# Three cost estimates of a list scheduler: GpSimd's splits and ScalarE's second-norm scaling

## Chip, cores and metric

The kernel runs on one core of one Trainium2 chip. The metric is the device time of one execution in microseconds, as the median of several runs. PE is TensorE, DVE is VectorE, ACT is ScalarE, POOL is GpSimd, SP is SyncE, which here only issues DMAs.

## What is computed

The input is 16 sequences of 256 tokens with 128 features, fp32. Twelve layers of linear attention (no softmax) with 16 heads of 8 features run one after another, then a layer norm, one gated feed-forward with a hidden width of 384, and a second layer norm.

```python
for i in range(12):
    q, k, v = split(x @ Wqkv[i].T + bqkv[i], 3)           # 16 heads of 8
    att = einsum('bhqd,bhkd->bhqk', q, k) / sqrt(8)
    y = einsum('bhqk,bhkd->bhqd', att, v)
    x = y @ Wproj[i].T + bproj[i] + x
x = layernorm(x0 + x)
h = silu(x @ wg.T) * (x @ wu.T)                            # wg, wu, wd: int weights / 127
x = layernorm(x + h @ wd.T)
```

## The kernel before

The 16 sequences are handled as 8 pairs (512 tokens each, tiles of 128 partitions), in two halves of 4 pairs. Because there is no softmax, the attention of a layer is carried as a 128x128 matrix for each sequence (`tst`, with two more columns, so 2x130 = 260 columns for a pair). In each layer a pair goes through `products` (k, v and q by matmuls), `heads` (small 32x32 products for a whole half) and `projection`. fp32 operands are split for the matmuls into a rounded high part and a low remainder. In `projection` ACT writes the high part `hi` (L543), and POOL subtracts it to make the low part `lo` (L544); both go into `thl`. The next layer's matmuls L434 to L444 read both parts. The weights of each layer are split in the same way into `whl`, with the low part on POOL (L299).

After the layers, `ffn` runs for each pair. There is a first norm; the transposed tokens are split into `xh` and `xl`; `whole` (L694) adds them up again for the residual, on ACT or POOL. For each of three blocks of 128 hidden features, PE makes the gate and up products (L706, L707), ACT the SiLU (L709), and DVE the product with `up` (L710). The result is rounded into `hh` (L713, ACT or DVE), the remainder `hl` is taken (L714, POOL or DVE), and both go into the down product (L719, L720). Then DVE adds the residual (L732), PE transposes (L736), and the second norm follows: DVE statistics (L618, L621, L623), POOL's power -0.5 and one product (L634, L636), ACT's scaling, four chunks of 128 tokens for a pair (L650), and the store (L743). The last pair is cut in two: DVE scales its first two chunks (L648), ACT the other two.

No order is written out by hand. Every step is an `Op` with a cost in nanoseconds for each engine that may do it. `Plan.run` makes a list schedule when the kernel is built: it keeps a time at which each engine comes free, takes for every ready step the engine on which it would be finished first, and issues, among the steps that could start first, the one with the lowest priority number. A step's result counts as ready some time after its end (`AFTER`, `TO_PE`). In the feed-forward, DVE's finish is counted 500 ns later than it is (`SPARE`):

```python
rank = t + c + (SPARE if e == DVE and o.prio > L - 1.6 else 0)
```

The instructions go to each engine's queue in the order that this plan gives, and on the chip each engine works through its queue in that order. An estimate therefore does nothing on the chip by itself: it can only move a step to another engine or to another place in a queue. The costs that matter here:

```python
def dve(n, fast=False):
    return 69 + n / (1.92 if fast else 0.96)
def act(n, sbuf=False, pointers=0):
    return (94 if sbuf else 51) + 93 * pointers + n / 1.2
op({POOL: pool(N), DVE: dve(N)}, ... sub(e, t(hlo), t(sg), t(hh)) ...)      # L714, N = 512
op({ACT: act(N), POOL: pool(N)}, whole, ...)                                # L694
```

`pool(n)` is used by the split of the weights (n = 512, once 128), by `thl`'s low part (260, POOL only), by the mask product of `heads` (L511, 256, DVE or POOL), by `whole` and by `hl` (512).

Of the kernel before, what the change touches and what calls it, by code (L numbers as in the profile page):

```python
# [21 lines left out]
C = 128  # L22
# [13 lines left out]
K = N // 128  # L36
# [37 lines left out]
PE, ACT, DVE, POOL, SP = "pe", "act", "dve", "pool", "sp"  # L74
# [100 lines left out]
# [6 lines that stand above are left out]


def pool(n):
    return 147 + 2.1 * n


def flat(t):
# [4 lines left out]
def linear_attention_ffn_kernel(ctx: ExitStack, tc: tile.TileContext, x, xt, wall, wq0, bias, wg, wu, wd, out):  # L192
# [86 lines left out]
    def prep_weights(l):  # L279
# [17 lines left out]

        after = [vlo[G - 1]] if l > 1 else []
        plan.op({POOL: pool(n)}, lambda e: sub(e, whl[hl.slot][:, 1, a:], wraw[raw.slot][:, a:], whl[hl.slot][:, 0, a:].bitcast(F32)), [raw, *after], [hl], prio)  # L299

        def turn(e):
# [176 lines left out]
    def heads(l, o, prio, riders):  # L478
# [26 lines left out]
        for lo, oo, _, pc, _ in more:  # L505
# [3 lines left out]
        plan.op({DVE: dve(OB * 32)}, lambda e: nc.vector.tensor_tensor(  # L509
            gm, bank(pm)[:, : OB * 32].rearrange("p (b j) -> p b j", j=32), kvo[:, o * OB : (o + 1) * OB], ALU.add), [pm, vkvo[o]], [vgm[o]], prio)  # L510
        plan.op({DVE: dve(OB * 32), POOL: pool(OB * 32)}, lambda e: mul(e, gm, gm, mask32.unsqueeze(1).to_broadcast([128, OB, 32])), [], [vgm[o]], prio)  # L511

        def mm_y(e):
# [7 lines left out]
    def projection(l, p, py, prio):  # L521

        _, whv, turned = wts[l]
        bs, r = slice(p * PB, (p + 1) * PB), p % G
        wp = lambda i: wpt[turned.slot][:, i, r - 1, :] if r else whl[whv.slot][:, i, 3 * C :]
        hi, lo, ts = thl[p][:, 0], thl[p][:, 1], flat(tst[:, bs, :])
        yh, yl = yhl[p][:, 0], yhl[p][:, 1]
        pw = Val("bank")
        plan.op({ACT: act(PB * W), DVE: dve(PB * W)}, lambda e: copy(e, yh, bank(py)[:, : PB * W]), [py], [vyh[p]], prio)
        plan.op({DVE: dve(PB * W)}, lambda e: nc.vector.tensor_tensor(yl, bank(py)[:, : PB * W], yh.bitcast(F32), ALU.subtract), [py, vyh[p]], [vyl[p]], prio)  # L530

        def mm_w(e):
            o = bank(pw)[:, : PB * W]
            nc.tensor.matmul(o, wp(1), yh, start=True, stop=False)  # L534
            nc.tensor.matmul(o, wp(0), yh, start=False, stop=False)  # L535
            nc.tensor.matmul(o, wp(0), yl, start=False, stop=(l < L - 1))  # L536
            if l == L - 1:
                nc.tensor.matmul(o, centerr, flat(hi), start=False, stop=False)
                nc.tensor.matmul(o, centerr, flat(lo), start=False, stop=True)
        plan.op({PE: (3 if l < L - 1 else 5) * mmr(PB * W)}, mm_w, [vyh[p], vyl[p], vhi[p], vlo[p], whv, turned], [pw, vw[p]], prio)  # L540
        plan.op({DVE: dve(PB * W)}, lambda e: nc.vector.tensor_tensor(ts, bank(pw)[:, : PB * W], ts, ALU.add), [pw], [vt[p], vc[p]], prio)  # L541
        if l < L - 1:
            plan.op({ACT: act(PB * W, True)}, lambda e: copy(e, flat(hi), ts), [vt[p], vc[p]], [vhi[p]], prio)  # L543
            plan.op({POOL: pool(PB * W)}, lambda e: sub(e, flat(lo), ts, flat(hi).bitcast(F32)), [vt[p], vc[p], vhi[p]], [vlo[p]], prio)  # L544
# [50 lines left out]
    def ffn(p, prio):  # L595
# [5 lines left out]
        v = {n: Val() for n in ("tt", "st", "rs", "x1", "xh", "xl", "sg0", "sg1", "hh0", "hh1", "hl0", "hl1")}  # L601

        def op(costs, emit, reads, writes):
            plan.op(costs, emit, reads, writes, prio)

        def norm(src, centred, other=None):


            xs, rows = t("x1"), lambda: bank(src)
            cut = lambda a, k: a[:, k * C : (k + 1) * C]  # L610
            row = lambda k: cut(bank(other if other and k >= K // 2 else src), k)

            def stats(e, ks=range(0, K, 2)):

                for k in ks:
                    b = bank(other if other and k else src)
                    both = b[:, k * C : (k + 2) * C].rearrange("p (k c) -> p c k", c=C)
                    nc.vector.bn_stats(t("st")[:, k : k + 2, :].rearrange("p k s -> p (k s)"), both)  # L618

            def var(e):  # L620
                nc.vector.tensor_scalar(t("ve"), t("st")[:, :, 2], 1.0 / C, EPS, ALU.mult, ALU.add)  # L621
                if not centred:
                    nc.vector.tensor_scalar(t("nm"), t("st")[:, :, 1], -1.0, None, ALU.mult)  # L623
            some, tiny = dve(2 * C) + 40, 75 * (2 - centred)
            if other:
                parts = [Val(), Val()]
                for k, b in ((0, src), (2, other)):
                    op({DVE: some}, lambda e, k=k: stats(e, [k]), [b], [parts[k // 2]])
                op({DVE: tiny}, var, parts, [v["st"]])
            else:  # L630
                op({DVE: K // 2 * some + tiny}, lambda e: (stats(e), var(e)), [src], [v["st"]])

            def rstd(e):
                nc.gpsimd.tensor_tensor(t("rs"), t("ve"), mhalf, ALU.pow)  # L634
                if not centred:
                    nc.gpsimd.tensor_tensor(t("nb"), t("nm"), t("rs"), ALU.mult)  # L636
            op({POOL: 1060 + 220 * (not centred)}, rstd, [v["st"]], [v["rs"]])

            def scale(e, ks=range(K)):
                if centred and e == DVE:  # L640
                    nc.vector.tensor_tensor(chunks(xs), chunks(rows()), t("rs").unsqueeze(2).to_broadcast([128, K, C]), ALU.mult)
                    return
                for k in ks:
                    d, r, rs = cut(xs, k), row(k), t("rs")[:, k : k + 1]
                    if centred:
                        nc.scalar.activation(d, r, AF.Copy, scale=rs)
                    elif e == DVE:
                        nc.vector.tensor_scalar(d, r, t("st")[:, k, 1:2], rs, ALU.subtract, ALU.mult)  # L648
                    else:
                        nc.scalar.activation(d, r, AF.Identity, bias=t("nb")[:, k : k + 1], scale=rs)  # L650
            if centred:
                costs = {DVE: dve(N), ACT: K * act(C, False, 1)}
            else:
                costs = {ACT: K * act(C, False, 2)}
            if not other:
                op(costs, scale, [src, v["rs"], v["st"]], [v["x1"]])
                return [v["x1"]]

            ends = [Val(), Val()]
            op({DVE: 2 * 319}, lambda e: scale(e, range(2)), [src, v["rs"], v["st"], v["x1"]], [ends[0]])  # L660
            op({ACT: 2 * act(C, False, 2)}, lambda e: scale(e, range(2, K)), [other, v["rs"], v["st"], v["x1"]], [ends[1]])
            return ends


# [7 lines left out]
        def mm_r(e):  # L672
            rows = cqs[p // G].unsqueeze(1).to_broadcast([128, 2, C])
            for b in range(PB):
                nc.tensor.matmul(bank(pr)[:, 2 * b * C : 2 * (b + 1) * C], pick[:, p % G * PB + b, :], rows, start=True, stop=False)
                for k in (2 * b, 2 * b + 1):
                    nc.tensor.matmul(bank(pr)[:, k * C : (k + 1) * C], x[:, k * 128 : (k + 1) * 128], t("tt")[:, b * C : (b + 1) * C], start=False, stop=(k % 2 == 1))
        op({PE: K * mm32() + PB * mmr(2 * C)}, mm_r, [vx[p], v["tt"], vcq[p // G], vpick], [pr])
        norm(pr, True)

        def tr_x(e):
# [48 lines left out]
        for (d, cols), o, r in zip(downs, outs, sums):  # L730
# [6 lines left out]
            op({PE: m // 128 * 109}, tr_o, [r], [o])  # L737
        po, po2 = outs if len(outs) == 2 else (*outs, None)
        ends = norm(po, False, po2)
        m = N // len(ends)  # L740
        for i, end in enumerate(ends):
# [59 lines left out]
```

## Time and profile before

| what | value |
|---|---|
| median of 3 runs | 305.5 us (305.44 to 306.06) |
| the profiled execution's own time | 305.16 us |
| its span, first to last instruction | 303.2 us |
| mean granted TensorE clock | 0.998 |
| busy in the span: PE | 294.3 us (97%) |
| DVE | 226.1 us (75%) |
| ACT | 217.7 us (72%) |
| POOL | 137.8 us (45%) |
| chain of work that ended last | PE 87%, DVE 10%, ACT 1%, issue 1% |

The span is what the instructions of one profiled execution cover; the execution's own time is 1.96 us longer than the span. The busy shares are means over stages with different limits: start (about 0 to 30 us), layers (to about 240 us), feed-forward (to about 298 us) and a last stretch without matmuls.

### The profile page before, as it was taken

How to read it: one execution, taken by the hardware profiler on the slowest of the kernel's cores; microseconds unless marked ns; L12 is line 12 of the kernel's file. 1: busy time of each engine (PE TensorE's matmuls, PEld its weight loads, DVE VectorE, ACT ScalarE, POOL GpSimd, SP SyncE). 2: the span in 40 equal slices, each digit the busy share in tenths (PEclk: the TensorE clock that was granted, in tenths of full speed). 3: DMA queues.
4: the chain of work that ended last, by engine and by line, in shares of the span. 5: the costliest groups of instructions: out<-in, count | busy, mean ns of one | idle time of the engine just before them, and what ended most of it. 6: DMA issues, size and time to landing. Idle time of an engine off the chain costs nothing.

```text
span 303.2 us, 12834 instructions
## 1 busy us (share of the span) xinstructions
PE 294.3 (97%) x5376; PEld 269.8 (89%) x5376; DVE 226.1 (75%) x683; ACT 217.7 (72%) x559; POOL 137.8 (45%) x208
## 2 busy tenths in 40 slices
PE   8999999999999999999999999999999999999981
PEld 8989999999999999999999999989999998878760
DVE  4796887777677676876767777786644789999993
ACT  3556877867777768777686666777887558788875
POOL 8256452334531445225432354224431167777883
PEclk9999999999999999999999999999999999999999
DMA  7624213112031120311302102120000000000225
GB/s 214 163 91 131 67 39 89 38 46 82 3 89 37 39 89 4 88 40 28 98 2 56 37 17 50 49 68 17 2 2 4 3 1 2 0 0 8 63 70 138
DMA packets 22489, 15.65 MB, mean 52 GB/s; under 512 B 1952, under 2 KB 19872, under 8 KB 22432
## 3 DMA queue, kind: packets, MB, share of 16 engines
q1 hardware_dynamic: 21872, 14.62, 17.3%
q8 instruction: 42, 0.69, 0.9%
q10 hardware_dynamic: 560, 0.22, 0.3%
q14 instruction: 15, 0.12, 0.1%
HBM read 8.02 MB, written 2.10 MB: 33 GB/s over the span
## 4 chain that ended last, share of the span: by engine, by line
PE 87%; DVE 10%; issue 1%; ACT 1%; POOLq 0%; POOL 0%; DVEq 0%
PE bank L455 14%; PE bank L434 8%; PE bank L517 8%; PE bank L436 7%; PE bank L435 7%; PE bank L442 5%; PE bank L499 5%; PE bank L536 4%; PE bank L534 4%; PE bank L535 4%; PE bank L443 3%; PE bank L444 3%; PE bank L336 3%; DVE st L618 2%; PE bank L706 2%; PE bank L707 2%
## 5 line engine op out<-in xcount | busy, mean ns | idle before, releaser
L210 POOL TENSOR_TENSOR thl<-tst,thl 128x260 fp32r<-128x260 f32 x88 | 64.8, 768 | 123.1 <-ACT thl L205 123.1
L205 ACT COPY qgv<-bank 128x256 f32<-128x256 f32 x169 | 59.8, 378 | 19.2 <-PE bank L444 12.9
L205 ACT COPY kv<-bank 128x512 f32<-128x512 f32 (+1 forms) x93 | 53.4, 575 | 19.5 <-PE bank L436 14.2
L434 PE MATMUL bank<-whl,thl 128*128 128x256 f32 x176 | 51.9, 295 | 0.0
L436 PE MATMUL bank<-whl,thl 128*128 128x256 f32 x176 | 49.7, 282 | 0.0
L435 PE MATMUL bank<-whl,thl 128*128 128x256 f32 x176 | 49.4, 281 | 0.0
L455 PE MATMUL bank<-kv,g 128*128 128x128 f32 x352 | 46.1, 275 | 0.0
L541 DVE TENSOR_TENSOR tst<-bank,tst 128x260 f32<-128x260 f32 x96 | 36.9, 425 | 9.4 <-PE bank L536 9.0
L205 ACT CAST thl<-tst 128x260 fp32r<-128x260 f32 x88 | 33.0, 408 | 14.6 <-DVE tst L541 14.5
L455 PEld LDWEIGHTS bank<-kv,g 128*128 128x128 f32 x352 | 42.7, 191 | 0.4 <-issue 0.4
L448 DVE TENSOR_SCALAR qgv<-bank,bcol 128x2 f32<-128x2 f32 x88 | 19.2, 221 | 28.3 <-ACT qgv L205 22.9
L434 PEld LDWEIGHTS bank<-whl,thl 128*128 128x128 f32 x176 | 33.1, 188 | 4.0 <-issue 3.8
L530 DVE TENSOR_TENSOR yhl<-bank,yhl 128x260 fp32r<-128x260 f32 x96 | 34.4, 420 | 2.2 <-ACT yhl L205 2.1
L436 PEld LDWEIGHTS bank<-whl,thl 128*128 128x128 f32 x176 | 33.1, 188 | 0.3 <-POOL thl L210 0.2
L435 PEld LDWEIGHTS bank<-whl,thl 128*128 128x128 f32 x176 | 33.2, 189 | 0.0
L442 PE MATMUL bank<-thl,whl 128*128 128x260 f32 x88 | 28.8, 327 | 0.0
L205 ACT CAST yhl<-bank 128x260 fp32r<-128x260 f32 (+1 forms) x61 | 21.8, 408 | 8.3 <-PE bank L517 7.7
L207 DVE CAST yhl<-bank 128x260 fp32r<-128x260 f32 (+1 forms) x43 | 16.7, 430 | 12.7 <-PE bank L517 12.7
L517 PE MATMUL bank<-qgv,gm 32*32 32x130 f32 x1536 | 25.8, 280 | 0.2 <-DVE gm L213 0.2
L443 PE MATMUL bank<-thl,whl 128*128 128x260 f32 x88 | 24.8, 282 | 0.0
L444 PE MATMUL bank<-thl,whl 128*128 128x260 f32 x88 | 24.7, 281 | 0.0
L517 PEld LDWEIGHTS bank<-qgv,gm 32*32 32x32 f32 x1536 | 17.2, 103 | 5.5 <-ACT kv L205 0.3
(157 smaller groups left out, 694.7 us busy)
## 6 DMA issues: line engine op xcount, KB each, us to landing
wraw<-wall SPq DMA_DIRECT2D x12, 256.0 KB, 3.0
wpt<-whl SPq DMA_DIRECT2D x24, 96.0 KB, 2.2
qgv<-x SPq DMA_DIRECT2D x8, 256.0 KB, 5.0
xt<-xt SPq DMA_DIRECT2D x8, 256.0 KB, 3.1
out<-kv SPq DMA_DIRECT2D x7, 256.0 KB, 2.3
wpt<-whl SPq DMA_DIRECT2D x24, 64.0 KB, 2.7
wpt<-whl SPq DMA_DIRECT2D x24, 32.0 KB, 1.9
wraw<-wg SPq DMA_DIRECT2D x1, 192.0 KB, 3.2
```

The costliest lines, as they stand in the source:

```text
L205: nc.scalar.copy(dst, src)
L210: (nc.vector if e == DVE else nc.gpsimd).tensor_tensor(dst, a, b, ALU.subtract)
L434: nc.tensor.matmul(o, hi[:, b, 0:C], hl(0, 1, 2), start=True, stop=False)
L435: nc.tensor.matmul(o, hi[:, b, 0:C], hl(1, 1, 2), start=False, stop=False)
L436: nc.tensor.matmul(o, lo[:, b, 0:C], hl(0, 1, 2), start=False, stop=True)
L442: nc.tensor.matmul(o, hl(0, 0), flat(hi), start=True, stop=False)
L443: nc.tensor.matmul(o, hl(0, 0), flat(lo), start=False, stop=False)
L444: nc.tensor.matmul(o, hl(1, 0), flat(hi), start=False, stop=True)
L455: nc.tensor.matmul(bank(pgv)[:, b * C : (b + 1) * C], g0[p][:, b, :], tv(b), start=True, stop=True)
L517: nc.tensor.matmul(bank(pys[r])[group(g + r), b * W : (b + 1) * W], gm[group(g), r * PB + b, :], qss[p][group(g), b, :], start=True, stop= ...
L530: plan.op({DVE: dve(PB * W)}, lambda e: nc.vector.tensor_tensor(yl, bank(py)[:, : PB * W], yh.bitcast(F32), ALU.subtract), [py, vyh[p]], [ ...
L541: plan.op({DVE: dve(PB * W)}, lambda e: nc.vector.tensor_tensor(ts, bank(pw)[:, : PB * W], ts, ALU.add), [pw], [vt[p], vc[p]], prio)
```

## The change

It replaces the straight line that stands for POOL's two-input splits by another one, and the estimate of ACT's scaling in the second norm, `act(128, False, 2)` = 343.7 ns a chunk, by 375 ns, and by 400 ns for the two chunks of the last pair. No step is added, removed or rewritten.

```diff
 def pool(n):
-    return 147 + 2.1 * n
+    return 135 + 2.4 * n
...
             else:
-                costs = {ACT: K * act(C, False, 2)}
+                costs = {ACT: K * 375}
...
             op({DVE: 2 * 319}, lambda e: scale(e, range(2)), [src, v["rs"], v["st"], v["x1"]], [ends[0]])
-            op({ACT: 2 * act(C, False, 2)}, lambda e: scale(e, range(2, K)), [other, v["rs"], v["st"], v["x1"]], [ends[1]])
+            op({ACT: 2 * 400}, lambda e: scale(e, range(2, K)), [other, v["rs"], v["st"], v["x1"]], [ends[1]])
```

## The prediction, made before the changed kernel was run

> **What bounds the kernel now.** I read the page's busy slices first, then the busy time by stage, then the chain that ended last over the final 17 us, then GpSimd's own order there.
>
> The busy slices, 7.6 us each, in tenths:
>
> ```profile
> PE   8999999999999999999999999999999999999981
> DVE  4796887777677676876767777786644789999993
> POOL 8256452334531445225432354224431167777883
> ```
>
> PE is full from the second slice on. DVE joins it only in the last eight slices, and there POOL is no longer half idle. The same by stage (the stretch, then PE, PE's weight loads, DVE, ACT and POOL):
>
> ```profile
> 30.00:240.00 210.00, 209.84 (x4542) 196.61 (x4541) 150.04 (x465) 154.45 (x407) 78.75 (x109) 1.00 0.16 43
> 240.00:286.50 46.50, 46.11 (x281) 39.24 (x280) 44.22 (x97) 35.90 (x86) 32.00 (x32) 1.00 0.03 8
> 286.50:298.00 11.50, 9.60 (x53) 7.09 (x51) 11.10 (x32) 9.61 (x24) 9.61 (x13) 1.00 0.32 88
> 298.00:303.20 5.20, 0.00 (x0) 0.00 (x0) 0.74 (x3) 1.67 (x5) 1.21 (x2) 0.87 0.55 151
> ```
>
> In the layers PE is idle 0.16 us of 210 at a full clock. No new order can gain there, and one that keeps PE fed loses nothing. From 240 to 286.5 us PE is idle 0.39 us. After that the binding engine changes: DVE is busy 11.10 of 11.50 us, PE only 9.60. The chain says so in words (start, duration, what):
>
> ```profile
> 286.63 1.28 DVE xt L710 x2
> 287.91 0.60 DVE xt L732
> 288.51 0.68 DVE st L618 x2
> ...
> 289.62 0.52 DVE hl L210
> 290.14 0.68 DVE qgv L710
> 290.82 0.60 DVE hl L210
> 291.42 0.60 DVE xt L732
> ```
>
> One DVE instruction follows the other; a 128x512 one advances the chain by 0.60 us. Two of these links are `hl` remainders that could as well have been POOL's. So the end is paid in DVE instructions: one more of 128x512 in this stretch costs 0.60 us, one less gains as much until PE or ACT is late. ACT's last run of scaling there is 12 chunks in 4.58 us from 294.29, ends at 298.87, and ACT then waits 0.47 us for POOL: it is the next one late, by half a microsecond.
>
> **What the estimates say, and what the chip does.** The groups of the split and of the scaling (min/median/max in ns for the tile queries of `hl` and of the scaling):
>
> ```profile
> L210 POOL TENSOR_TENSOR hl<-xt,hh x8: 1288/1300/1732, 255.2 to 287.0; 128x512 fp32r<-128x512 f32 x8
> L210 POOL TENSOR_TENSOR hl<-qgv,hh x7: 1279/1304/1684, 259.5 to 291.5; 128x512 fp32r<-128x512 f32 x7
> L210 DVE TENSOR_TENSOR hl<-xt,hh x7: 676/681/1801, 260.8 to 290.7; 128x512 fp32r<-128x512 f32 x7
> ```
>
> At 512 elements POOL takes 1300 ns. The old estimate, 147 + 2.1*512 = 1222, is 78 short; the new one, 135 + 2.4*512 = 1364, is 64 too long. At 260 elements the old one gives 693 and the new one 759; four of these splits in a row take 3.03 us in the layers (127.02 to 130.05), 757 each. So the new line follows the trace in the layers, where nothing depends on it, and in the feed-forward it only trades one error for an equal one of the other sign.
>
> **The change, part by part.** It adds and removes no instruction. Its cost on the chip is what the list does with it.
>
> *thl's low parts, 88 on POOL alone, 66 ns dearer each.* Four in a row are counted 264 ns later. In a steady layer the fourth ends at 130.05 and the first k, v product of the next layer starts at 130.68, 0.63 us after it; 264 fits into that, so PE's order there should stay. What covers it is the other half's q products (128.13 to 130.2); if that cover were gone, the price would be 0.26 us a half. Only at the first layer, where four splits take 3.32 us from 22.31 and PE works right behind them (9.78 of 10 us busy between 20 and 30), can the order change: between -0.22 (that idle time filled) and +0.26 (264 ns waited once). I take nothing.
>
> *The weights' low parts (142 dearer, POOL alone) and the mask product (685 to 749, DVE at 336 or POOL).* The weights are split a layer ahead, with POOL idle 5 us and more around them (5.61 us before 127.02): nothing. The mask product's 4 that are on POOL could go to DVE, 435 ns each at 75% load: nothing.
>
> *ACT's second-norm scaling: 4*343.7 = 1375 becomes 1500, and 687 becomes 800.* The trace has 1.50 us for four and 4.58 for twelve, 0.81 for the last two: the new estimates are right. No other engine may do this step, so only what stands behind it in ACT's list moves: 125 ns later a pair. ACT is busy 9.61 of 11.5 us at the end and waits for POOL there. Between -0.1 and +0.1 by order; I take nothing.
>
> *hl's remainders and `whole`, 142 dearer each.* This is the part that can move work. DVE's due is 69 + 512/0.96 = 602, plus the handicap of 500: with both engines free, POOL at 1222 loses to 1102, and wins where DVE is taken for some time. I carried the list's rule through with the old costs: POOL's lead over DVE in its 15 remainders is 204 ns at least. So 142 alone moves none. Where two stand back to back, the second is charged 284. That is so at one place, as GpSimd's order in time shows:
>
> ```profile
> 286.83 0.20 POOL L636 TENSOR_TENSOR nb<-nm,rs 128x4 f32<-128x4 f32 x1
> 286.98 1.29 POOL L210 TENSOR_TENSOR hl<-xt,hh 128x512 fp32r<-128x512 f32 x1
> 288.22 1.30 POOL L210 TENSOR_TENSOR hl<-qgv,hh 128x512 fp32r<-128x512 f32 x1
> ```
>
> There the list's lead for the second was 205 ns, less than 284: it goes to DVE. 288 us lies inside the DVE-bound end, so it adds a link to the chain: +0.60 us. It can cost more. A DVE remainder has two inputs in SBUF, and one of them met POOL:
>
> ```profile
> 260.80 1.80 DVE L210 TENSOR_TENSOR hl<-xt,hh 128x512 fp32r<-128x512 f32 x1
> 260.77 1.28 POOL L693 TENSOR_TENSOR kv<-yhl,thl 128x512 f32<-128x512 f32 x1
> ```
>
> It took 1.80 us for 0.68, and the next DVE instruction started 1.72 us after it instead of 0.60. So a moved remainder costs 0.60 at least and 1.72 if POOL happens to start just before it; I take 0.60, since 7 of the 8 on DVE ran at 676 to 693.
>
> The Trainium skill, "SBUF — State Buffer", section "Who interferes with whom", states this as a rule: a DVE instruction with two SBUF inputs contends with a GpSimd one that reads SBUF, and the later one blocks fully. It speaks against the change: at a busy POOL it would price the moved remainder at the 1.72 of the pair above, and the sum would be +1.7.
>
> *Sum.* The profiled execution took 305.16 us (span 303.2 and 1.96 around it); with +0.60 it would take 305.76. The median of the runs is 0.34 above the profiled execution, so I forecast 306.1.
>
> **The rivals.**
>
> *Given back (not slower).* With the remainder of 288.22 gone, POOL is free 1.3 us earlier, and the next remainder, which DVE does at 290.74, may come back to POOL: in the list DVE had it by only 115 ns, while DVE itself is now 602 later. Then DVE has as many links as before: 305.5, between 305.2 and 305.9. For it: the small lead. Against it: that one belongs to the last pair, 1.30 us on POOL where DVE needs 0.68, and POOL's idle time before 291.55 is short. It decides if the list's ready time of that remainder lies within about 0.6 us of POOL's.
>
> *Faster.* `whole` at 260.77 was POOL's by 305 ns in the list, directly behind a remainder: it is now charged 284, so 21 ns more of any delay send it to ACT, which stands idle 1.59 us until 266. Then the 1.80 us of DVE become 0.68: -1.12 on DVE. Of that PE can use only its 0.39 idle us before 286.5; the rest counts if DVE keeps the lead to the end. Time: 305.5 less 0.4 to 1.1, 304.4 to 305.1.
>
> *Two links or a blocked one.* Besides the one above, `hh` casts (ACT or DVE, 0.43 on DVE) lean to DVE as ACT is counted dearer; two remainders give +1.2, one with a blocked one 0.60 + 1.72 = 2.3: 306.7 to 307.8.
>
> *PE starved.* A later due of `hl` lets PE take other products first, and they hold the eight PSUM banks; the down product then comes late. PE has no spare time before 286.5, so each wait counts in full; beyond 307.8.
>
> **How the numbers follow.** A measurement of this kernel can tell about 0.2% (0.6 us) from no change, so the border lies at 306.1. One link on DVE: 0.28, of which 0.18 over the border and 0.10 under it. Two or a blocked one: 0.17. Starved PE: 0.07. Given back: 0.24. Faster: 0.24. That gives slower 0.18 + 0.17 + 0.07 = 0.42, same 0.10 + 0.24 = 0.34, faster 0.24. The range from 304.4 to 307.8 takes in all but the starved case and what the faster case holds below its price. The likeliest case's own range is 305.9 to 306.5.
>
> **What would show it.** Right: the layers take the same time (PE idle under 0.3 us between 30 and 240); 14 `hl` remainders on POOL and 9 on DVE, the new one near 288 us; DVE over 11 us busy of the last 11.5 before its final statistics, which come 0.6 us later. Wrong: 15 and 8 as before (given back); `whole` once instead of twice on POOL and no DVE remainder above 1 us (faster); PE idle by more than 0.5 us between 240 and 286 us, or a layer that lost its cadence of about 9.7 us a half, which would refute the reasoning on the layers.

## The result, and the profile after

The changed kernel takes 306.76 us (median, 305.8 to 307.66) against 305.51 us for the kernel before, measured in turns: a ratio of 1.004 with a 95% interval from 1.0027 to 1.0053. It is slower by 1.25 us. The forecast was 306.1 us with a range from 304.4 to 307.8.

The busy slices of the profile after (the span is 304.9 us):

```profile
PE   8999999999999999999999999999999999999971
DVE  4796777777777676776767777786544789999993
POOL 8255353334541345314442254323431176767783
```

The picture is the same as before. By stage (the stretch, then PE, PE's weight loads, DVE, ACT and POOL; the third stretch starts 0.3 us later, as the end does, and stops where POOL's last power starts, 298.02 before and 299.71 now):

```profile
30.00:240.00 210.00, 209.66 (x4537) 196.23 (x4535) 150.68 (x464) 153.62 (x404) 78.92 (x109) 1.00 0.16 43
240.00:286.80 46.80, 46.41 (x294) 39.44 (x282) 44.16 (x97) 36.24 (x86) 32.28 (x33) 1.00 0.03 8
286.80:299.70 12.90, 10.01 (x53) 7.09 (x51) 12.49 (x32) 9.77 (x25) 9.65 (x13) 1.00 0.28 79
299.70:304.90 5.20, 0.00 (x0) 0.00 (x0) 0.73 (x3) 1.58 (x5) 1.21 (x2) 0.70 0.55 151
```

PE is idle 0.34 us of 210 in the layers (0.16 before) and 0.39 us from 240 on, as before. From the last power on, the same 5.2 us follow. The third stretch, 11.50 us before, is 12.90 now. DVE is busy in it for 12.49 us, with the same 32 rows as before. So the time is in the DVE-bound end, and it isn't in more instructions. The `hl` remainders:

```profile
L210 POOL TENSOR_TENSOR hl<-xt,hh x8: 1281/1302/1748, 255.5 to 290.0; 128x512 fp32r<-128x512 f32 x8
L210 POOL TENSOR_TENSOR hl<-qgv,hh x7: 1283/1303/1687, 259.8 to 293.2; 128x512 fp32r<-128x512 f32 x7
L210 DVE TENSOR_TENSOR hl<-xt,hh x7: 674/684/1800, 261.1 to 292.5; 128x512 fp32r<-128x512 f32 x7
L210 DVE TENSOR_TENSOR hl<-qgv,hh x1: 691/691/691, 273.3 to 273.3; 128x512 fp32r<-128x512 f32 x1
```

15 on POOL and 8 on DVE, as before. But they are not the same ones. In the chain that ended last (start, duration, what) stands, 17 us before the end, a remainder that was not on DVE before:

```profile
287.57 1.59 DVE hl L210
289.16 0.60 DVE xt L710
289.76 0.60 DVE xt L732
290.36 0.68 DVE st L618 x2
...
292.57 0.61 DVE hl L210
...
293.26 0.60 ACT xt L709
293.86 1.41 ACT kv L650 x4
...
295.30 0.64 PE bank L736 x4
```

The other 128x512 links on DVE still advance it by 0.60. This one took 1.59. The timeline after, DVE and POOL (start, duration, engine, line, what; in brackets idle time and what ended it):

```profile
287.32 1.29 POOL L210 TENSOR_TENSOR hl<-qgv,hh 128x512 fp32r<-128x512 f32 x1
287.57 1.59 DVE L210 TENSOR_TENSOR hl<-xt,hh 128x512 fp32r<-128x512 f32 x1
...
289.99 1.30 POOL L210 TENSOR_TENSOR hl<-xt,hh 128x512 fp32r<-128x512 f32 x1 [1.38 <-ACT hh L205]
...
293.19 1.28 POOL L210 TENSOR_TENSOR hl<-qgv,hh 128x512 fp32r<-128x512 f32 x1
293.88 0.62 DVE L621 TENSOR_SCALAR ve<-st 128x4 f32<-128x4 f32 x1
```

Each of the two long DVE instructions begins inside a split of POOL's and ends 0.03 to 0.55 us after it: 0.91 us over the usual 0.68, and 0.45 over the variance's usual 0.17. Before, POOL's two splits of 286.98 to 289.52 (shown in the prediction) stood over these:

```profile
286.63 1.28 DVE L710 SCALAR_TENSOR_TENSOR xt<-bank,xt 128x512 f32<-128x512 f32 x2
287.83 0.68 DVE L732 SCALAR_TENSOR_TENSOR xt<-bank,kv 128x512 f32<-128x512 f32 x1
288.43 0.75 DVE L618 BATCH_NORM_STATS2 st<-bank 128x6 f32<-128x256 f32 x2
289.21 0.34 DVE L621 TENSOR_SCALAR ve<-st 128x4 f32<-128x4 f32 x1
...
289.54 0.68 DVE L210 TENSOR_TENSOR hl<-xt,hh 128x512 fp32r<-128x512 f32 x1
```

Those that read a PSUM bank kept their time; the variance, which reads SBUF alone, took 0.34 for 0.17; the remainder came just behind the splits. The Trainium skill, "SBUF — State Buffer", section "Who interferes with whom", says which is which: a DVE instruction with two SBUF inputs contends with a GpSimd one that reads SBUF, `tensor_scalar` can too in its two-port mode, and one with at most one SBUF input outside these modes does not. The rows agree: L210 at 0.68 or 1.59, L621 at 0.17 or 0.62 (in which mode it ran no row tells), the whole profile before has no 128x512 instruction of L710 or L732 above 0.693, and none of L618 above 0.433.

**Why the remainders changed places.** `Plan.run` can be followed without the chip. The pairs are counted from 0, so pair 7 is the last. With the old estimates, ACT's cast of pair 5's last block ends at 287.623 us in the list's time, and its remainder could start 0.160 later, at 287.783, before POOL comes free at 287.887. Both it and pair 6's remainder could then start there, and pair 5, being earlier, went first. With scaling at 1500 ahead of it, and all else as it was, the cast ends 125 ns later, and its remainder is ready at 287.908: 21 ns too late (with the new line for POOL too, both times are 66 ns later and the 21 ns the same). POOL takes pair 6's. Pair 5's goes to DVE, and later another one of pair 6's goes from DVE to POOL: an exchange. In the list with the new scaling estimates alone, these two are the only ones of 1906 steps that change engine. On the chip there is no such 21 ns: in the profile after, pair 5's cast ended at 287.18, before POOL came free at 287.37.

**A measure for the runs.** The profiles' starts differ (an unchanged layer program reaches the feed-forward between 244.8 and 246.7 us), so profiles are compared from the first variance instruction (L621) to the end of the span; and POOL's last six powers (L634) mark the DVE-bound part, without the last scalings and stores: from the first to the last of them 12.35 us before (285.67 to 298.02) and 13.70 after (286.01 to 299.71). The difference, 1.35, is 0.91 + 0.45 - 0.09 (an earlier variance took 0.25 for 0.34) + some 0.1 in the last transposes.

### The profile page after: what moved, and what is told of

It reads as the page before. It is cut to its first block, busy times and chain, and to the rows that moved or that the text cites. A ratio compares the mean times of both kernels' runs of the same rounds, so it can differ in the third digit from the quotient of the medians.

```text
span 304.9 us, 12847 instructions
## 1 busy us (share of the span) xinstructions
PE 294.8 (97%) x5376; PEld 269.9 (89%) x5376; DVE 228.6 (75%) x684; ACT 217.5 (71%) x557; POOL 138.2 (45%) x209
## 4 chain that ended last, share of the span: by engine, by line
PE 79%; DVE 15%; ACT 2%; issue 2%; POOLq 0%; DVEq 0%; POOL 0%; ACTq 0%
PE bank L455 14%; PE bank L517 8%; PE bank L434 8%; PE bank L435 7%; PE bank L436 7%; PE bank L442 5%; PE bank L499 5%; PE bank L536 4%; PE bank L534 4%; PE bank L535 4%; PE bank L443 3%; PE bank L444 3%; DVE xt L710 3%; PE bank L336 3%; DVE st L618 2%; DVE hl L210 2%
## 5 line engine op out<-in xcount | busy, mean ns | idle before, releaser
L210 POOL TENSOR_TENSOR thl<-tst,thl 128x260 fp32r<-128x260 f32 x88 | 64.6, 766 | 123.7 <-ACT thl L205 123.7
```

The lines of the kernel that those rows point to most:

```text
L210: (nc.vector if e == DVE else nc.gpsimd).tensor_tensor(dst, a, b, ALU.subtract)
```

## The experiments

Medians in us, beside those of the kernel before in the same series. The last two columns are the two measures just given.

| run | median | before | ratio (95%) | first variance to end | first to last power |
|---|---|---|---|---|---|
| before | | | | 58.4 | 12.35 |
| after | 306.76 | 305.51 | 1.004 (1.0027 to 1.0053) | 59.8 | 13.70 |
| e1 splits' line alone | 305.78 | 305.88 | 0.9991 (0.9977 to 1.0005) | 58.4 | 12.37 |
| e2 scaling alone | 307.14 | 305.88 | 1.004 (1.0025 to 1.0055) | 59.8 | 13.71 |
| e10 the same, another series | 307.1 | 305.71 | 1.0049 (1.003 to 1.0067) | 59.7 | 13.71 |
| e6 375 alone | 306.87 | 305.56 | 1.0044 (1.0028 to 1.006) | 59.8 | 12.27 |
| e7 400 alone | 305.51 | 305.56 | 1.0 (0.9982 to 1.0017) | 57.7 | 12.37 |
| e12 exchange alone | 307.64 | 305.76 | 1.0059 (1.0038 to 1.008) | 60.3 | 14.00 |
| e11 exchange undone | 306.65 | 305.76 | 1.0033 (1.0016 to 1.005) | 59.3 | 13.21 |
| e3 remainder later | 307.49 | 305.88 | 1.0048 (1.003 to 1.0065) | 59.8 | 13.72 |
| e5 later still | 306.75 | 305.56 | 1.005 (1.0031 to 1.0069) | 59.3 | 13.27 |
| e9 no wait left | 306.48 | 305.71 | 1.0025 (1.001 to 1.004) | 59.2 | 12.27 |
| e4 sum on ACT | 305.49 | 305.88 | 0.9987 (0.9969 to 1.0005) | 58.3 | 12.36 |
| e8 `nm` on POOL, sum on ACT | 305.23 | 305.56 | 0.9987 (0.9973 to 1.0001) | 58.0 | 12.09 |

The fifth column, less before's 58.4, follows the medians' differences within 0.4 us in all but e7, whose one profile is 0.7 us shorter than before's where its median shows no gain.

### Which estimate: e1, e2, e10

```diff
 def pool(n):
-    return 147 + 2.1 * n
+    return 135 + 2.4 * n      # e1: this alone
...
-                costs = {ACT: K * act(C, False, 2)}
+                costs = {ACT: K * 375}      # e2, e10: these two alone
-            op({ACT: 2 * act(C, False, 2)}, ...
+            op({ACT: 2 * 400}, ...
```

> Only GpSimd's estimate is new (135+2.4n); ScalarE's scaling keeps 343.7 ns a chunk. The list then gives the layers in the order of the changed kernel and the last 20 us in the order of the kernel before. My theory now: the loss lies in the last 20 us and comes from ScalarE's estimate, so this run is within 0.4 us of before (the changed trace was 0.09 us late after 70 us and 0.34 us late at 245 us): 305.3 to 305.9. The prediction's own step, that GpSimd's dearer splits move a remainder at the end, would make it 0.6 us or more slower.

> Only ScalarE's scaling estimate is new (375 and 400); GpSimd keeps 147+2.1n. The layers are those of before, instruction by instruction; at the end a remainder of pair 5 goes from GpSimd to VectorE and one of pair 6 from VectorE to GpSimd, as in the changed kernel. My theory: all of the loss, +1.0 to +1.4 us (306.5 to 306.9), final statistics about 1.3 us later, pair 5's remainder on VectorE near 287 us taking about 1.6 us. Rival (the layers' new order or GpSimd's estimate costs it): within 0.3 us of before.

The splits' line alone is no change that can be told; the scaling alone costs as much as the whole change. In e2 the long remainder (1.58 us) and the long variance (0.62) are there as in the profile after. e10 repeats it in another series:

> The kernel with ScalarE's estimate alone once more, for a comparison on the same chip in the same call: 306.6 to 307.2, ratio 1.003 to 1.005 by every theory.

### Which of the two scalings: e6, e7

e6 keeps the 375 alone, e7 the 400 alone.

> Only the estimate of 375 ns is new, the last pair's chunks keep 343.7. By its instruction order this kernel has the same exchange near 288 us (pair 5's remainder on VectorE, pair 6's on GpSimd) and a slightly different order before it. Theory of the exchange: slower by 1.0 to 1.4 us, 306.7 to 307.4. Rival (any new order at the end costs about the same, or the 400 is what costs): unlike that.

> Only the estimate of 400 ns for the last pair's two chunks is new. The order changes at 263 to 280 us, but the exchange near 288 us is not there: pair 5's remainder stays on GpSimd, pair 6's on VectorE. Theory of the exchange: within 0.4 us of before, 305.4 to 306.2. Rival (any new order costs): slower by 1 us or more.

The 375 alone makes the exchange and costs the same 1.3 us; the 400 alone moves other steps and costs nothing that can be told, so not every new order of this end costs time. But in e6 the DVE waits near 288 are absent, and the powers take 12.27 us:

```profile
288.27 0.68 DVE L210 TENSOR_TENSOR hl<-xt,hh 128x512 fp32r<-128x512 f32 x1
...
297.15 5.00 ACT L650 ACTIVATE kv<-bank,nb,rs 128x128 f32<-128x128 f32 x14 [0.97 <-POOL nb L636]
```

Of the 1.4 us that e6's profile is longer from the first variance on, 1.0 came out behind the powers: ACT's last scaling is one run of 14 chunks that ends at 302.15, and the span ends at 305.8, 6.2 us after the last power began (5.2 before). The other 0.4 lies before the first of the six powers. Nor does e6 need the tie of 21 ns: in its list pair 5's cast stands one SiLU earlier and ends at 287.271, DVE comes free first and wins the remainder by 462 ns, and four other remainders change engine as well. So e6 shows that such a loss can arise in another place than DVE, as e9 below does, but not that the exchange alone made it there.

### The exchange by itself: e12, e11

Both take the finished order of the list and change where two steps stand: `replay` gives out the same steps in the same order, but with a step put behind another one (the pairs of numbers) or on another engine. 1817 is pair 5's remainder, 1854 pair 6's. e12, on the old estimates:

```diff
-    plan.run()
+    plan.run(); replay(plan, [(1817, 1852), (1854, 1853)], {1817: "dve", 1854: "pool"})
```

> All estimates are the old ones; in the order of before the exchange alone is made by hand: pair 5's remainder goes from GpSimd to DVE behind pair 6's last gate, pair 6's from DVE to GpSimd ahead of its second power. Theory (the exchange is the loss): a DVE remainder near 288 of 1.4 to 1.8 us, GpSimd's second split waits over 1 us for ACT's cast, 306.3 to 307.1, ratio 1.0025 to 1.005. Rival (the loss needs the moved steps on ACT and PE): 305.4 to 306.0.

It costs 1.88 us, more than the change and more than either expectation:

```profile
288.01 1.30 POOL L210 TENSOR_TENSOR hl<-qgv,hh 128x512 fp32r<-128x512 f32 x1
288.26 1.60 DVE L210 TENSOR_TENSOR hl<-xt,hh 128x512 fp32r<-128x512 f32 x1
...
292.19 1.56 POOL L210 TENSOR_TENSOR hl<-xt,hh 128x512 fp32r<-128x512 f32 x1 [2.89 <-ACT hh L205]
...
297.05 0.69 DVE L710 SCALAR_TENSOR_TENSOR xt<-bank,xt 128x512 f32<-128x512 f32 x1 [0.75 <-ACT xt L709]
```

The exchange alone makes the long remainder. POOL then waits 2.89 us for ACT's cast, and the pair's power stands behind that split; with ACT's order unadapted, DVE later waits 0.75 more. So the exchange is enough for a loss, of which the long remainder is one part. e11, on the new scaling estimates, undoes it:

```diff
-    plan.run()
+    plan.run(); replay(plan, [(1817, 1816), (1854, 1883)], {1817: "pool", 1854: "dve"})
```

> Only ACT's two scaling estimates are new, and in the finished order the exchange alone is undone: pair 5's remainder goes to GpSimd directly behind its power at 286, pair 6's to DVE behind the last multiplication of pair 7; everything else keeps the order that the new estimates gave. Theory (the exchange is the loss): no DVE remainder over 0.7 us and no variance instruction over 0.4 us after 286, the first to the last of GpSimd's last six powers 12.1 to 12.6 us, 305.3 to 306.0, ratio 0.999 to 1.0015. Rival (the loss lies in the other places that the new estimates moved on ACT and PE): still 306.6 to 307.3.

The expectation failed: 0.9 us slower than before, where e2 and e10 are 1.3 and 1.4 slower; the intervals overlap, so that anything came back is not shown by the medians. The first long remainder and the long variance are gone, but

```profile
290.96 1.28 POOL L210 TENSOR_TENSOR hl<-qgv,hh 128x512 fp32r<-128x512 f32 x1
291.35 1.44 DVE L210 TENSOR_TENSOR hl<-xt,hh 128x512 fp32r<-128x512 f32 x1
...
292.88 0.60 ACT L709 ACTIVATE xt<-bank 128x512 f32<-128x512 f32 x1 [2.00 <-DVE hl L210]
```

Pair 7's remainder, which the new estimates had also placed two instructions later, now meets POOL's third split; the 0.76 us that it is held are most of the 0.86 that the powers took longer than before. So the exchange is enough, but taking it back is not: the rest of the order no longer keeps DVE's remainders out from under the splits.

### Moving the remainder away: e3, e5, e9

On the scaling estimates of e2, the remainder on DVE is moved behind other instructions of the same queue, out from under the first split: e3 behind pair 4's residual, e5 behind pair 3's statistics, e9 as e5 with pair 7's remainder behind pair 4's statistics.

```diff
-    plan.run()
+    plan.run(); replay(plan, [(1817, 1782)], {})                   # e3
+    plan.run(); replay(plan, [(1817, 1740)], {})                   # e5
+    plan.run(); replay(plan, [(1817, 1740), (1877, 1784)], {})     # e9
```

> As the run with ScalarE's estimate alone, but in VectorE's queue pair 5's remainder stands two instructions later, behind two that read PSUM, so that it starts after GpSimd's split of pair 6 has ended; same engines, same number of instructions on each. Theory of the blocked instruction: the remainder takes 0.68 us instead of 1.6, and 0.9 us of the loss comes back: 305.4 to 306.0. Rival (the swap costs by its order on TensorE and by whom it makes wait, not by the block): no more than 0.3 us comes back.

The remainder took 0.68, and nothing came back:

```profile
290.16 1.30 POOL L210 TENSOR_TENSOR hl<-xt,hh 128x512 fp32r<-128x512 f32 x1 [1.38 <-ACT hh L205]
290.33 1.16 DVE L621 TENSOR_SCALAR ve<-st 128x4 f32<-128x4 f32 x1
```

The next variance, 0.17 us of work, waited in its place for 0.99.

> As the run with ScalarE's estimate alone, but pair 5's remainder on VectorE now stands behind pair 3's statistics, variance and negative mean. In the run that put it two places later the remainder took 0.68 us, and the wait came back 1.4 us later as a variance instruction of 1.16 us under GpSimd's next split. Theory (VectorE's instructions with SBUF operands wait while GpSimd's split holds what both read through; the sum of such waits is the loss): here the remainder and that variance both end before GpSimd's split starts, so 0.9 us comes back, 306.0 to 306.6, and GpSimd's split waits 0.4 instead. Rival (VectorE's waits are a symptom, and TensorE's or ScalarE's order sets the time): no more than 0.3 us comes back, 306.8 to 307.5.

In e5 the first wait went to POOL's side (its split took 1.55), and the powers take 0.44 us less than in e2. The medians don't show that: 1.19 us slower than before, for 1.26 in e2, between the theory and its rival. A variance of 1.07 us for 0.17, under the next split, stands in the way:

```profile
292.65 1.28 POOL L210 TENSOR_TENSOR hl<-qgv,hh 128x512 fp32r<-128x512 f32 x1
292.89 1.07 DVE L621 TENSOR_SCALAR ve<-st 128x4 f32<-128x4 f32 x1
```

> As the run before it with pair 5's remainder behind pair 3's statistics, and now also pair 7's remainder behind pair 4's statistics, variance and negative mean. In that run the first wait was gone, 0.45 us of 1.35 came back in the profile's last 20 us, and pair 4's variance waited 1.07 us under GpSimd's split of pair 7. The exchange of the remainders stays. Theory (the loss is the sum of VectorE's waits under GpSimd's splits): no variance and no remainder on VectorE above 0.7 us after 286 us, the last statistics within 0.3 us of where before has them against the start of this stretch, 305.5 to 306.1, at least 0.7 us better than the kernel with ScalarE's estimate alone in the same call. Rival (the exchange costs otherwise, or TensorE and ScalarE become late as these remainders come later): 306.6 to 307.2, no better than it.

In e9 no remainder after 286 is above 0.69 us on DVE, no variance above 0.18, and the powers take 12.27 us, as before. Still only 0.6 us of e10's 1.4 came back, less than the theory asked for and more than its rival allowed. Its timeline:

```profile
290.34 0.17 DVE L621 TENSOR_SCALAR ve<-st 128x4 f32<-128x4 f32 x1
...
290.78 1.55 POOL L210 TENSOR_TENSOR hl<-xt,hh 128x512 fp32r<-128x512 f32 x1 [1.38 <-ACT hh L205]
292.29 1.01 POOL L634 TENSOR_TENSOR rs<-ve,mhalf 128x4 f32<-128x4 f32 x1
...
294.10 0.60 ACT L709 ACTIVATE xt<-bank 128x512 f32<-128x512 f32 x1 [1.67 <-PE bank L736]
...
296.58 5.00 ACT L650 ACTIVATE kv<-bank,nb,rs 128x128 f32<-128x128 f32 x14 [0.49 <-POOL nb L636]
```

The variance is there at 290.51, but POOL's power on it starts at 292.29, behind the split of the exchange, which had waited 1.38 us for ACT's cast. So the pairs reach ACT late and close together: its last 14 chunks are one run of 5.00 us that ends at 301.58, 2.51 us after the last power began (2.12 before), and the span ends 3.5 us after ACT's run (3.1 before), with the last stores close together. These two differences make the 0.8 us that e9 is slower than before. This is read from the profile and not tested apart: no run put that power ahead of the split.

### Less DVE work in the order of before: e4, e8

e4 gives `whole` of pair 4 to ACT, and e8 does that and moves the negated mean of the second norm to POOL.

```diff
-    plan.run()
+    plan.run(); replay(plan, [], {1760: 'act'})      # e4, e8
...
-                    nc.vector.tensor_scalar(t("nm"), t("st")[:, :, 1], -1.0, None, ALU.mult)      # e8
+                None if centred else nc.gpsimd.tensor_scalar(t("nm"), t("st")[:, :, 1], -1.0, 0.0, ALU.mult, ALU.add)
```

> The kernel before with one step moved: the sum of high and low part of pair 4, at 260.8 us on GpSimd, goes to ScalarE, at the same place of the order. VectorE's remainder at 260.8 us then meets no GpSimd split and takes 0.68 us instead of 1.80. The prediction's faster rival: 0.4 to 1.1 us faster than before, 304.4 to 305.1. If a VectorE saving that early is lost because TensorE bounds until 286 us: within 0.2 us of before; if ScalarE becomes late by its extra 0.6 us: slower by up to 0.6.

The 1.80 us remainder at 260.8 became 0.68, as the prediction's "faster" case wanted, but DVE lost time again 2 us later, and the run is not told from no change:

```profile
261.06 0.68 DVE L210 TENSOR_TENSOR hl<-xt,hh 128x512 fp32r<-128x512 f32 x1
...
262.88 1.29 POOL L210 TENSOR_TENSOR hl<-qgv,hh 128x512 fp32r<-128x512 f32 x1 [1.81 <-DVE hh L207]
263.20 1.52 DVE L210 TENSOR_TENSOR hl<-xt,hh 128x512 fp32r<-128x512 f32 x1 [0.40 <-PE bank L677]
```

DVE waited 0.40 us for PE, which binds there, and the next remainder met the split that POOL began at 262.88.

> The kernel before, in its own order, with two edits: the sum of pair 4 on ScalarE (as in the earlier run), and the negative mean of the second norm computed on GpSimd just ahead of its power instead of on VectorE, beside the variance there. VectorE loses 8 instructions, 0.08 to 0.15 us each, of which 5 lie in the last 12 us where it is the bound. Theory: 0.4 to 0.8 us faster than before, 305.0 to 305.5; GpSimd takes 0.2 us more a pair. Rival (GpSimd's longer chain to the scaling becomes late, or the saving only meets GpSimd's splits sooner): within 0.2 us of before, or slower by up to 0.5.

e8 shortened the powers' stretch by 0.26 us. Its ratio's interval reaches 1.0001, so it is not told from no change either. No kernel of this study beats the one before by more than can be measured.

## Why the prediction held, and where it failed

The time lies in the range, and slower was the likeliest of the three outcomes; but that the range held is luck. The forecast of 306.1 came from a term for `hl` that e1 shows to be nothing, and the time of 306.76 from a term that had been put at nothing. By the prediction's own sign, 15 and 8 remainders as before, its likeliest case was wrong.

- *Layers and PE before 286: held.* PE's idle time is 0.34 and 0.39 us (0.16 and 0.39 before). The 0.34 is just over the 0.3 that the prediction had set as a sign, but e1, which has the same estimate for the layers, isn't slower.
- *The end is paid in DVE time: held for the changed kernel.* The 1.35 us lie there, with DVE busy for 12.49 of 12.90 us. In e6 and e9 the loss came out mostly behind the powers, so it doesn't hold for every order.
- *thl, the weights, the mask and hl's 142 ns: nothing was the right value for all of them together* (e1: between -0.7 and +0.2 us). For `hl` the prediction had taken +0.60. That term was wrong: it compared a lead of 205 ns, taken from a finished order, with 284. At that moment DVE would indeed be ahead by 78 in e1's list, but pair 3's statistics can start on DVE then too, go first by their priority, and POOL's lead becomes 823. In e1 the second of the two back-to-back splits stayed on POOL (288.66, 1.31 us).
- *"I take nothing" for ACT's scaling: this is the step that failed.* It was bounded by ±0.1 us, with the reason that no other engine may do the step, "so only what stands behind it in ACT's list moves". What stands behind it was the cast that releases a split, and 125 ns made it 21 ns late for POOL. The term measured +1.26 us (e2) and +1.39 (e10).
- *The link's price: 0.60 or, met by POOL, 1.72.* The exchange kept the number of links, and what it cost was the second kind of price: 0.91 and 0.45 us of waiting. Of the prediction's cases, "given back" had the count right (15 and 8) with no loss, and "a blocked one" the mechanism. The lead of 115 ns that "given back" leaned on was misread: it belongs to pair 7's remainder, at 289.54; the one at 290.74 is pair 6's, and DVE had it by 395 in the list. The Trainium skill's rule, weighed there at +1.7 us in all though for another remainder, was nearer to what the end shows than the +0.60 that was taken; 7 of 8 undisturbed remainders were no evidence for a remainder that is moved to where POOL works back to back.
- *What stays open.* That the losses of e6, e9 and e11 (1.3, 0.8 and 0.9 us) have different places is seen in their profiles; no run removes all of them at once under the new estimates, so what the exchange must cost in a better order around it is not known. That the two engines wait for one another at SBUF is inferred from times: after 286 us, every remainder and every variance that is long on DVE, in all fourteen profiles, lies over a split, and the instructions that read a bank are not long there.

## What to carry to other kernels

An estimate nearer to the trace doesn't make a list's order better: the list of before, with scaling 8% too cheap, happened to lay GpSimd's two splits near 288 us over VectorE instructions mostly fed by PSUM, and in the changed kernel 21 ns of the list's time ended that. For a change of estimates, look for ties: which steps become ready within the change of some engine's free time, also on engines that the changed step doesn't use. And price a moved VectorE instruction with SBUF operands by what GpSimd does at its new place; if one such wait is cleared, look which instruction comes under the split next before counting the gain.

## What the runs showed of the hardware

A VectorE instruction need not be large to be held: the variance over 128x4 elements, 0.17 us, took 0.62 (after), 1.07 (e5) and 1.16 us (e3), each under a GpSimd split of 1.28 to 1.30 us that had begun 0.17 to 0.69 us earlier. It goes both ways: where VectorE's remainder had begun first, the split took 1.55 us for 1.29 (e5, e9). GpSimd's small steps are held like that too, in the kernel before as well. This power over 128x4 elements takes 1.01 us elsewhere, and VectorE's remainder of 289.54 had begun first:

```profile
289.63 1.45 POOL L634 TENSOR_TENSOR rs<-ve,mhalf 128x4 f32<-128x4 f32 x1
```

And a wait that is cleared can move to the next instruction with SBUF operands: in e3, e4, e5 and e11 it did, and of the three on the new scaling estimates only e11's median suggests that a part came back (0.4 to 0.5 of e2's and e10's 1.3 to 1.4 us, within the intervals).
